# Written orders for the end of the attention and the gating, and normalised rows turned through memory and VectorE

## The chip, the cores and the metric

One core of one Trainium2 chip runs the whole program in one launch. The metric is the device time in microseconds (us). The kernel before was run three times: 1278.26, 1278.86 and 1281.36 us, with a median of 1278.86. One further execution was profiled.

The engines are called PE (TensorE), DVE (VectorE), ACT (ScalarE), POOL (GpSimd) and SP (SyncE, which here only issues DMAs). Each engine executes its own instructions in order, and waits in that order.

## What is computed

The input is `x` of 4 x 16 x 16 x 1024, that is 1024 tokens of 1024 channels (float32). Two layers follow each other:

```
x = x + conv_attn(group_norm(x))          # layer 0: q, k, v, a 256x256 map per head and batch
t = tokens(x)                             # 4 x 256 x 1024
t = t + attention(layer_norm(t))          # layer 1: 16 causal heads, then W_proj and b_proj
h = layer_norm(t)
g = softmax(h @ gate_w + gate_b)          # 8 experts
w = g * (g >= 0.1); w = w / sum(w)
t = t + sum_e w[:, e] * (h @ expert_w[e] + expert_b[e])
```

So there are two layer norms over tokens, and after each the rows are needed transposed: channels on the partitions, tokens along the free axis, since a matrix product on PE contracts over the partitions.

## The kernel before

The 1024 tokens are eight tiles of 128 (`NT = 8`, `P = 128`), and the 1024 channels are eight chunks (`NC = 8`). Everything is float32. A matrix product with 512 columns is recorded as two 128x512 matmul records of 0.43 us each, so that one step over a chunk takes 0.86 us of PE. Unless something else is said, the order of the instructions on each engine is chosen by the scheduler of the framework, which may move an instruction ahead of others. Inside `tc.manual_schedule()` the order of the text is the order on each engine; with a set of engines given, only for these.

**End of layer 0 (lines 432 to 453).** For each of eight tiles `content` makes one part of the map (matmuls `pc`, line 342, added on DVE in line 350), and 16 matmul records `py` (line 443) multiply it with the values; DVE adds `py` onto the tile of x (line 450). Then `layer_norm` (line 155): statistics on DVE, a root on ACT, the normalised row written by ACT (line 166), eight transposes on PE (line 170) into PSUM, and two ACT copies of these into `ln1` (line 171), which is the transposed operand of the next layer. POOL adds the bias `bp` (line 452), and SP writes the row to `x_rows` in memory, from where it comes back later.

**Attention (lines 457 to 703).** `project_v` makes the values from `ln1`. Two-by-two block products with seven instead of eight multiplications are used here and for q and k: DVE makes sums of blocks first (`sums_of_A`, `sums_of_B`), and PE then makes the seven products `pqk` (line 492). The heads go in eight pairs, and four batches make 32 steps `(pair, b)`. A step consists of:

- `scores` (line 573): four matmuls into the one buffer `sc`; DVE adds the mask and writes `s` (line 593), two maxima on DVE (line 605), four exponentials on ACT, the reciprocal of their sums on DVE (line 614), four products on POOL (line 617). SP then writes the weights, laid out by quarters, to memory (line 623) and reads them back in four pieces (line 627).
- three steps later (`lag = 3`) `turned` (line 632): one DVE transpose by blocks of 32x32, which together with the trip through memory gives the full transpose; and `values` (line 638), eight matmul records, with a bias added on DVE into `y_T` (line 651).

Into these steps the dictionary `units` places the products of the next pair's q and k, and `out_at` places six pieces of the output projection `project_out` (line 658, matmuls `po` in line 663, added onto x on DVE in line 666) in steps 28 to 33. In step 27 eight reads `x_rows` to `xb` go out on SP (line 697). The whole loop is in the scheduler's order.

**Gating (lines 797 to 1028).** The ten other pieces of the output projection, 80 chunks of 0.86 us, run while the rows of x go through a chain of stages, which the dictionary `after` places by halves of pieces: `normalise` (stage 0: statistics, root, the row on DVE in line 863, eight transposes on PE in line 845, a copy of one half on ACT and of the other on DVE, and a write of the row, laid out by quarters, to `rows`, from which the experts' rows are gathered), `gate` (stage 1: 16 matmul records `parts` for the gates, a copy, a matmul `pg`, and some ten small DVE instructions with one exponential on ACT), `place` (stage 2: the place of each token in its experts' lists) and `enter` (stage 3: matmuls into `lists`). SP writes x to `out` after stage 0. Before the stages, DVE makes a number of constants (lines 804 to 839), and SP issues the two halves `w0` of the first expert's weights, 2 MB each, and its bias (lines 984 and 985). At the end `read_lists` turns the list of expert 0 into addresses.

**Experts (from line 1194 on).** This stage has a written order already. The last tile is multiplied by expert 0 as a whole (`weighted`, line 750, called `dense`), while POOL gathers the rows of the first list by indirect DMAs (line 735), DVE turns them by `turn` (line 745), and then the products of the experts follow.

Of the kernel before, what the change touches and what calls it, by code (L numbers as in the profile page):

```python
# [32 lines left out]
F32 = mybir.dt.float32  # L33
I32 = mybir.dt.int32
AF = mybir.ActivationFunctionType
ALU = mybir.AluOpType
# [31 lines left out]
def kernel(  # L68
# [86 lines left out]
    def layer_norm(ln, t, dst):  # L155
# [8 lines left out]
        less = small.tile([P, 1], F32, tag="ln_less", name=f"ln1_less{t}")  # L164
        nc.vector.scalar_tensor_tensor(less, mv[:, 0:1], -1.0, rstd, ALU.mult, ALU.mult)
        nc.scalar.activation(ln, xs[t], AF.Identity, bias=less, scale=rstd)  # L166
        for j in range(2):
            pt = tr(f"ln1_pt{t}_{j}")
            for c in range(4):
                nc.tensor.transpose(pt[:, ts(c, P)], ln[:, (4 * j + c) * P : (4 * j + c + 1) * P], ident)  # L170
            nc.scalar.copy(dst[:, 4 * j : 4 * j + 4, ts(t, P)], pt.rearrange("p (c n) -> p c n", c=4))


    with ExitStack() as layer0:
# [253 lines left out]
        ln1 = big_tile(1, "ln1")  # L428
        ln_rows = wpool.tile([P, 4, C], F32, tag="w", name="ln_rows")
        bp = ln_rows[:, 3, :]  # L430
        nc.gpsimd.dma_start(bp, b_proj.partition_broadcast(P))
        for i, (b, nt) in enumerate(tiles):
            if i == 0:
                content(b, nt)
            if i + 1 < NT:
                content(*tiles[i + 1])
            t = 2 * b + nt
            for hp in range(2):
                py = mm(f"py{t}_{hp}")
                for hl in range(2):  # L440
                    bh = b * HEADS0 + 2 * hp + hl
                    for mh in range(2):
                        nc.tensor.matmul(  # L443
                            py[:, ts(hl, M)],
                            s0[:, mh, ts(nt, S2), :, bh].rearrange("p i j -> p (i j)"),
                            v_T[:, mh, ts(b, M)],
                            start=(mh == 0),
                            stop=(mh == 1),
                        )
                nc.vector.tensor_add(xs[t][:, ts(hp, HALF)], xs[t][:, ts(hp, HALF)], py)  # L450
            layer_norm(ln_rows[:, i % 3, :], t, ln1)
            nc.gpsimd.tensor_add(xs[t], xs[t], bp)  # L452
            nc.sync.dma_start(x_rows[ts(t, P), :], xs[t])
# [3 lines left out]
    with ExitStack() as attention:  # L457
# [41 lines left out]
        def project_v(r):  # L499
# [18 lines left out]
            for t in range(4):  # L518
                nc.scalar.copy(homes(t)[1], one(t, 3, s4, b22))
# [829 lines left out]
```

## Time and profile before

| | |
|---|---|
| runs | 1278.26, 1278.86, 1281.36 us |
| profiled execution, its own time | 1278.4 us |
| its span | 1276.6 us |
| mean granted clock of PE | 0.991 |
| PE, DVE busy | 98%, 54% of the span |
| ACT, POOL busy | 17%, 27% |
| q1 (the queue of the plain loads and writes) | 27.3% of 16 engines' span |
| end of layer 0, gating | about 224 to 293 us, about 690 to 780 us |

The profile is of one execution. Its span, from the first to the last instruction, lies 1.8 us below the time of that execution. A line such as `L845 PE MATMUL row_pt<-ident,row ... x64 | 9.4, 295 | 4.9 <-DVE row L863 4.9` is a group: line of the kernel, engine, operation, what it writes and reads, how many, then busy time in us and the mean of one in ns, then the idle time of the engine just before these instructions and what ended it. Times of matmuls overlap, so a mean in ns is not what one of them costs on a full PE. A row of the windows gives start:end, length, busy time of each engine with the number of instructions, the granted clock of PE (1.00 is full), the share of the DMA engines and their GB/s. In the chain of waits each row has a start, a length, and the engine and line, or the DMA, that held the end back.

### The profile page before, as it was taken

The numbers are of one execution on the slowest core, as the hardware profiler recorded it, in microseconds if no ns is written. First come the engines' busy times: TensorE is split into PE (matmuls) and PEld (weight loads), VectorE is DVE, ScalarE is ACT, GpSimd is POOL, SyncE is SP. The second block draws the span as 40 slices with busy tenths as digits, with TensorE's granted clock in tenths as the row PEclk, the third lists the DMA queues.
The fourth block names the chain that finished last, engine by engine and source line by source line (L and its number), as shares of the span: only waits on it lengthen the run. The fifth ranks groups of instructions, "written<-read, shape, count | busy, mean of one in ns | idle before, by whom it ended". The sixth has DMA issues, their size and how long they took to land.

```text
span 1276.6 us, 12809 instructions
## 1 busy us (share of the span) xinstructions
PE 1248.8 (98%) x4646; PEld 657.0 (51%) x4646; DVE 694.6 (54%) x1297; ACT 221.6 (17%) x520; POOL 350.0 (27%) x423
## 2 busy tenths in 40 slices
PE   9999999999999999999889998999999999999997
PEld 5444895788884444444434544444344434433443
DVE  5784220566322666665545754755656665665642
ACT  3300111231000222222221322011111110111110
POOL 0000051230000222222210011554644544363520
PEclk9999999999999999999889998999999999999999
DMA  9020022612202535353744415274658375557442
GB/s 353 7 66 2 16 63 70 232 65 99 67 1 66 153 102 163 108 168 99 246 137 154 174 50 210 71 232 89 185 150 232 90 231 154 141 118 210 99 82 51
DMA packets 83605, 159.76 MB, mean 125 GB/s; under 512 B 8368, under 2 KB 39104, under 8 KB 83536
## 3 DMA queue, kind: packets, MB, share of 16 engines
q1 hardware_dynamic: 70704, 119.49, 27.3%
q0 software_dynamic: 12832, 39.39, 14.0%
q8 instruction: 38, 0.62, 0.2%
q14 instruction: 31, 0.25, 0.1%
HBM read 109.30 MB, written 45.35 MB: 121 GB/s over the span
## 4 chain that ended last, share of the span: by engine, by line
PE 75%; issue 13%; POOL 5%; DVE 3%; DMA 3%; ACT 0%; SPq 0%; POOLq 0%; ACTq 0%; DVEq 0%
PE p L1120 29%; PE po L663 7%; PE pq L259 7%; PE pv L492 7%; POOL s_q L617 5%; PE left L1162 3%; PE pT L378 3%; PE pqk L492 3%; PE py L443 2%; PE pk L321 2%; PE pc L342 2%; PE pv L403 2%; PE rest L1176 2%; PE last_pe L1274 1%; DMA s_rows<-s_q 1%
## 5 line engine op out<-in xcount | busy, mean ns | idle before, releaser
L735 POOL DMA_INDIRECT w_e_xg<-rows,gather x146 | 155.2, 1063 | 67.5 <-issue 41.7
L1120 PE MATMUL p<-w_e,A 128*128 128x512 f32 x368 | 163.2, 593 | 1.8 <-DVE slot L981 1.8
L617 POOL TENSOR_TENSOR s_q<-s_q,total 128x128 f32<-128x128 f32 (+1 forms) x128 | 65.3, 541 | 301.9 <-DVE total L614 301.9
L663 PE MATMUL po<-w_p,y_T 128*128 128x512 f32 x256 | 119.5, 613 | 0.0
L1120 PEld LDWEIGHTS p<-w_e,A 128*128 128x128 f32 x368 | 69.6, 190 | 90.4 <-issue 89.9
L1120 PE MATMUL p<-T,S 128*128 128x512 f32 x256 | 112.7, 593 | 0.0
L1126 ACT ACTIVATE y<-y,slot 128x512 f32<-128x512 f32 x64 | 46.0, 721 | 336.3 <-DVE y L1134 183.9
L763 POOL DMA_INDIRECT out_dram<-y,add x32 | 57.4, 1794 | 171.0 <-ACT y L1126 110.1
L259 PE MATMUL pq<-w_q,xn 128*128 128x512 f32 x224 | 99.6, 596 | 1.4 <-DVE q_s L263 1.1
L607 ACT ACTIVATE s_q<-s,top 128x256 f32<-128x256 f32 (+1 forms) x128 | 56.6, 443 | 182.6 <-issue 143.1
L492 PE MATMUL pqk<-ln,w_qk 128*128 128x512 f32 x192 | 86.0, 596 | 0.0
L1120 PEld LDWEIGHTS p<-T,S 128*128 128x128 f32 x256 | 48.6, 190 | 60.8 <-issue 60.7
L663 PEld LDWEIGHTS po<-w_p,y_T 128*128 128x128 f32 x256 | 47.5, 195 | 52.1 <-issue 51.9
L745 DVE STREAM_TRANSPOSE A<-w_e_xg 128x1024 f32<-128x1024 f32 x32 | 39.6, 1238 | 59.8 <-DMA w_e_xg<-rows,gather 56.6
L259 PEld LDWEIGHTS pq<-w_q,xn 128*128 128x128 f32 x224 | 41.8, 190 | 51.8 <-issue 47.4
L492 PE MATMUL pqk<-T,S_qk 128*128 128x512 f32 x128 | 58.3, 598 | 0.0
L492 PEld LDWEIGHTS pqk<-ln,w_qk 128*128 128x128 f32 x192 | 35.8, 190 | 42.7 <-issue 41.5
L1120 PE MATMUL p<-w_e,S 128*128 128x512 f32 x128 | 57.5, 592 | 0.0
L1120 PE MATMUL p<-T,A 128*128 128x512 f32 x128 | 57.5, 592 | 0.0
L492 PE MATMUL pv<-w_v,ln 128*128 128x256 f32 x192 | 43.4, 379 | 0.0
L1162 PE MATMUL left<-w_e,one 128*32 128x512 f32 x312 | 41.8, 593 | 0.0
L452 POOL TENSOR_TENSOR x_at<-x_at,ln_rows 128x1024 f32<-128x1024 f32 x8 | 19.4, 2429 | 76.6 <-ACT ln_rows L166 76.6
(265 smaller groups left out, 1781.0 us busy)
## 6 DMA issues: line engine op xcount, KB each, us to landing
w_e<-in_expert_w_dram SPq DMA_DIRECT2D x16, 2048.0 KB, 12.2
s_rows<-s_q SPq DMA_DIRECT2D x32, 384.0 KB, 2.5
s_rows<-s_rows SPq DMA_DIRECT2D x128, 96.0 KB, 2.4
w_qk<-in_W_attnT_dram SPq DMA_DIRECT2D x8, 1024.0 KB, 6.1
xn<-in_xT_dram SPq DMA_DIRECT2D x8, 512.0 KB, 5.8
x_at<-in_x_dram SPq DMA_DIRECT2D x8, 512.0 KB, 8.5
w_v<-in_W_attnT_dram SPq DMA_DIRECT2D x2, 2048.0 KB
x_rows<-x_at SPq DMA_DIRECT2D x8, 512.0 KB, 2.7
```

The lines of the kernel that those rows point to most:

```text
L259: nc.tensor.matmul(pq, xn[:, c, ts(t, P)], w_q[kc][:, c, :], start=(c == 0), stop=(c == NC - 1))
L378: nc.tensor.matmul(out_T[:, g, :, :], window[:, kc, :, :].rearrange("p i j -> p (i j)"), q0[:, kc, first : first + n_i, nj, :], start=(kc ...
L492: nc.tensor.matmul(bank, stationary(c), moving(c), start=(c == 0), stop=(c == NC // 2 - 1))
L607: nc.scalar.activation(blocks(h, qt), s[:, h, cols].rearrange("p (b f i) -> p b f i", f=Q, i=32), AF.Exp, bias=top[:, qt, h : h + 1], accu ...
L617: nc.gpsimd.tensor_mul(blocks(h, qt), blocks(h, qt), total[:, qt, h : h + 1].unsqueeze(2).unsqueeze(3).to_broadcast([P, 1 + qt, Q, 32]),)
L663: nc.tensor.matmul(po, y_T[:, c, ts(t, P)], w_p[j][:, c, :], start=(c == 0), stop=(c == NC - 1))
L735: nc.gpsimd.indirect_dma_start(out=row[:, g, :], out_offset=None, in_=table[: (TOK - P) * Q, :] if e in SHORT else table, in_offset=bass.I ...
L745: nc.vector.transpose(row_T[:, :, :slots].rearrange("p c (g j) -> p g c j", j=32), row[:, : slots // 32, :].rearrange("p g (c i) -> p g c ...
L763: nc.gpsimd.indirect_dma_start(out=out[: TOK - P, :] if e in SHORT else out, out_offset=bass.IndirectOffsetOnAxis(ap=add[:slots, e, k : k ...
L1120: nc.tensor.matmul(bank, a[:, c, :], b[:, c, :], start=(c == 0), stop=(c == NC // 2 - 1))
L1126: nc.scalar.mul(y[i][:, ts(j, HALF)], y[i][:, ts(j, HALF)], slot[:, e, 1, 2 * pair + i : 2 * pair + i + 1])
L1162: nc.tensor.matmul(bank[ts(i, 32), :], stationary, w[of][j][:, c, :], start=(c == 0), stop=(c == NC - 1))
```

## The change

Four things change.

1. **Layer 0.** `layer_norm` no longer transposes on PE. ACT writes the normalised row in the order of quarters, SP writes it to memory and reads it back by `quarters_of` in four pieces, and one DVE `turn` puts it into `ln1`. The write of `x_rows` moves from SP to POOL's queue. In this loop SP's instructions are in the written order. `project_v` takes the tiles in the order 1, 3, 0, 2 for products 1, 2 and 3, and its sums wait for the last tile's normalisation.
2. **Attention, steps 22 to 34.** They are in a written order on all engines. The scores of a step are split: `scores` ends with the exponentials, `scored` holds the rest. The sums of pair 7 (`sums_qk`) are made in step 22, units stand ahead of or behind the values and scores, the pieces of the output projection take the values and scores after their seventh chunk, the second half of `w_p` is loaded in step 28, and the reads of x are issued from POOL, two per step in steps 28 to 31.
3. **Gating.** It is in a written order on all engines, and `after` counts single chunks. For tiles 0 to 5 the row is written by ACT in quarter order, goes to memory and back by `quarters_of`, and is turned on DVE; tiles 6 and 7 keep the transposes on PE. The stages are six: `normalise`, `turn_rows`, `gate_sums`, `gate`, `place`, `enter`.
4. **Between gating and experts.** The address list is spread by PE before the last tile's statistics are made, 14 matmuls whose result is not used stand behind that, and the dense tile takes the stages of tile 7 and two sums of blocks of the weights between its chunks.

The diff, cut to its core:

```diff
+    def normalised(row, of, mean, rstd):
+        less = small.tile([P, 1], F32, tag="ln_less", name="ln_less")
+        done = nc.vector.scalar_tensor_tensor(less, mean, -1.0, rstd, ALU.mult, ALU.mult)
+        nc.scalar.activation(
+            row.rearrange("p (f c i) -> p c f i", f=Q, c=NC),
+            of.rearrange("p (c f i) -> p c f i", c=NC, f=Q),
+            AF.Identity, bias=less, scale=rstd)
+        return done
+
+    def quarters_of(rows, home, name):
+        row = home.tile([P, Q, C // Q], F32, tag="xg", name=name)
+        for f in range(Q):
+            nc.sync.dma_start(row[ts(f, 32), :, :], rows[:, f, :].rearrange("(g j) c -> j g c", j=32))
+        return row
...
-    def layer_norm(ln, t, dst):
+    def layer_norm(ln, t, dst, home, turns):
...
-        nc.scalar.activation(ln, xs[t], AF.Identity, bias=less, scale=rstd)
-        for j in range(2):
-            pt = tr(f"ln1_pt{t}_{j}")
-            for c in range(4):
-                nc.tensor.transpose(pt[:, ts(c, P)], ln[:, (4 * j + c) * P : (4 * j + c + 1) * P], ident)
-            nc.scalar.copy(dst[:, 4 * j : 4 * j + 4, ts(t, P)], pt.rearrange("p (c n) -> p c n", c=4))
+        done = normalised(ln, xs[t], mv[:, 0:1], rstd)
+        rows = turns.tile([P, Q, C // Q], F32, tag="rows", name=f"ln1_rows{t}")
+        nc.sync.dma_start(rows.rearrange("n f c -> n (f c)"), ln)
+        turn(dst[:, :, ts(t, P)], quarters_of(rows, home, f"ln1_quarters{t}"))
+        return done
...
+        with tc.manual_schedule(engines={mybir.EngineType.SP}):
...
+                ln_done = layer_norm(ln_rows[:, i % 3, :], t, ln1, tpool, turns)
+                nc.gpsimd.tensor_add(xs[t], xs[t], bp)
+                nc.gpsimd.dma_start(x_rows[ts(t, P), :], xs[t])
...
+            with tc.issue_after(ln_done.ins):
+                sums_of_A(*a, s1, s2, s4)
...
+        units = {
+            22: ([(6, 4), (6, 5)], []),
+            23: ([], [(7, 1)]),
+            24: ([(7, 2)], [(7, 6)]),
+            25: ([(7, 7), (7, 4)], []),
+            26: ([(6, 3)], [(7, 5)]),
+            27: ([(7, 3)], []),
+        }
+        out_at = {28: (0, 0), 29: (1, 0), 30: (0, 1), 31: (1, 1), 32: (2, 0), 33: (2, 1)}
+        with tc.manual_schedule():
+            for i in range(written, len(steps) + lag):
+                if i == written:
+                    w_p.append(w_tile("w_p0", W_projT[:, :HALF]))
+                if i == 28:
+                    w_p.append(w_tile("w_p1", W_projT[:, HALF:]))
...
+                if 28 <= i < 32:
+                    for t in range(2 * (i - 28), 2 * (i - 28) + 2):
+                        nc.gpsimd.dma_start(xs[t], x_rows[ts(t, P), :])
+                s_T = turned(*steps[i - lag], soft.pop(i - lag))
+                ahead, behind = units.get(i, ((), ()))
+                for unit in ahead:
+                    project_qk(*unit)
+
+                def values_and_scores():
+                    values(*steps[i - lag], s_T)
+                    return scores(*steps[i]) if i < len(steps) else None
+
+                made = []
+                if i in out_at:
+                    project_out(*out_at[i], {NC - 2: lambda: made.append(values_and_scores())})
+                else:
+                    made.append(values_and_scores())
+                if i == written:
+                    sums_qk(7)
+                for unit in behind:
+                    project_qk(*unit)
+                if made[0]:
+                    soft[i] = scored(*steps[i], *made[0])
...
-            nc.vector.tensor_scalar(row, xs[t], mv[:, 0:1], rstd, ALU.subtract, ALU.mult)
+            if t < NT - 2:
+                normalised(row, xs[t], mv[:, 0:1], rstd)
+                nc.sync.dma_start(rows[ts(t, P), :], row)
+                row = quarters_of(rows[ts(t, P), :].rearrange("n (f c) -> n f c", f=Q), l2w, f"quarters{t}")
+            else:
+                nc.vector.tensor_scalar(row, xs[t], mv[:, 0:1], rstd, ALU.subtract, ALU.mult)
+            nc.sync.dma_start(out[ts(t, P), :], xs[t])
+            return row
...
         after = {
-            0: (0, 2, 4, 6),
-            1: (2, 4, 6, 8),
...
+            0: (1, 11, 13, 14, 19, 24),
+            1: (3, 20, 22, 23, 28, 33),
+            2: (12, 29, 31, 32, 37, 42),
+            3: (21, 38, 40, 41, 46, 51),
+            4: (33, 47, 49, 50, 55, 60),
+            5: (49, 59, 61, 62, 67, 72),
+            6: (65, 69, 71, 72, 76, 79),
         }
...
+        with tc.manual_schedule():
+            for t in range(3, NT):
+                for j in range(2):
+                    project_out(t, j, {c: one_more for c in range(NC)})
+            entries = copy_lists(0)
+            pc = spread_lists(0, entries)
+
+            warm = tr("warm")
+            for _ in range(14):
+                nc.tensor.matmul(warm[:, :P], before, ones, start=True, stop=True)
+            stage(0, NT - 1)
+            take_lists(0, 1, pc)
+            stage(1, NT - 1)
...
-            first_sum(0)
-            second_sum(0)
-            bias_step(0)
...
-                {0: lambda: stage(2, NT - 1), 1: lambda: (put(0, 0), put(0, 1), row_sums(0, 0))},
+                {
+                    (0, 3): lambda: stage(2, NT - 1),
+                    (0, 4): lambda: (stage(3, NT - 1), first_sum(0)),
+                    0: lambda: (stage(4, NT - 1), put(0, 0)),
+                    (1, 3): lambda: put(0, 1),
+                    1: lambda: (row_sums(0, 0), second_sum(0), bias_step(0)),
+                },
```

## The prediction

> **What bounds the kernel now.** I read the busy shares, then the slices with the granted clock, then the windows around the places where the clock drops, then the groups of the instructions that leave, and last the chain of waits.
>
> ```profile
> PE 1248.8 (98%) x4646; PEld 657.0 (51%) x4646; DVE 694.6 (54%) x1297; ACT 221.6 (17%) x520; POOL 350.0 (27%) x423
> ...
> PEclk9999999999999999999889998999999999999999
> ```
>
> PE is busy 98% of the span, so only two things can pay: fewer PE instructions, and the places where PE waits or runs at a low clock. The digits 8 mark the second kind. The windows (length, then busy time of PE, PEld, DVE, ACT, POOL, then the granted clock, DMA share, GB/s) show them closely:
>
> ```profile
> 620.00:630.00 10.00, 5.95 (x34) 3.21 (x34) 7.18 (x13) 3.72 (x16) 3.34 (x8) 0.97 0.52 171
> 630.00:640.00 10.00, 10.00 (x26) 4.42 (x27) 3.08 (x6) 1.86 (x8) 2.35 (x5) 0.69 1.00 339
> ...
> 655.00:660.00 5.00, 3.44 (x11) 1.70 (x12) 3.83 (x7) 3.09 (x9) 2.05 (x5) 0.50 0.46 141
> 660.00:690.00 30.00, 30.00 (x91) 13.03 (x91) 9.07 (x19) 0.46 (x3) 1.56 (x4) 1.00 0.23 78
> ...
> 782.00:790.00 8.00, 6.89 (x32) 4.12 (x33) 4.05 (x15) 1.63 (x2) 0.00 (x0) 0.57 1.04 391
> ```
>
> PE stands still and then computes at half clock. By the matmul records the half clock holds three times for 6.83 us (629.36, 653.25, 782.96), each time after some 3 to 4 us of idle. Against the rate of undisturbed stretches (0.86 us for one 128x512 product step, which is two records of 0.43) I count 8.0 us lost at 624-636, 7.6 at 650-660, 8.2 at 778-791, 1.4 at 694-697 and 1.5 near 290. All other stretches are packed to within 0.2 us per change of shape.
>
> The instructions that leave PE:
>
> ```profile
> L845 PE MATMUL row_pt<-ident,row 128*128 128x128 f32 x64 | 9.4, 295 | 4.9 <-DVE row L863 4.9
> L170 PE MATMUL ln_pt<-ident,ln_rows 128*128 128x128 f32 x64 | 8.5, 275 | 1.4 <-ACT ln_rows L166 1.4
> ```
>
> Their busy time overlaps; in the chain of waits eight of them take 0.87 to 0.93 us, 0.11 us each. The 4.9 us beside the first group is PE waiting for a normalised row.
>
> The chain between 617 and 656 names what held PE in the attention:
>
> ```profile
> 626.49 5.51 DMA xb<-x_rows
> ...
> 634.01 9.03 DMA s_rows<-s_q
> ...
> 655.54 0.98 DVE s_T L632
> ```
>
> The eight 512 KB loads of x (626 to 634) and the weighted rows of the scores share SP's queue; a trip that otherwise takes 2.3 us took 9.03, so the values came late.
>
> **A, the end of layer 0.** Removed: 64 transposes x 0.109 = 7.0 us of PE, 16 ACT copies (0.59 each, beside PE), and PE's wait for the last row, 1.5. Added per tile, all beside PE: a 512 KB write, four quarter reads, a turn on DVE. Nearest rows:
>
> ```profile
> L745 DVE STREAM_TRANSPOSE A<-w_e_xg 128x1024 f32<-128x1024 f32 x32 | 39.6, 1238 | 59.8 <-DMA w_e_xg<-rows,gather 56.6
> ...
> s_rows<-s_rows SPq DMA_DIRECT2D x128, 96.0 KB, 2.4
> ...
> x_rows<-x_at SPq DMA_DIRECT2D x8, 512.0 KB, 2.7
> ```
>
> The trip of a row: ACT 1.24, write 2.7, four issues some 1.75 and landing 2.4, turn 1.24, about 9.3 us. PE's tile falls from 7.86 us (3.44 pc, 3.55 py, 0.87 transposes) to 6.99. DVE's tile is six 0.69 us instructions for adds and statistics and 0.7 of small ones, 4.8; with the turn 6.06 of 6.99. So DVE fits at 87%, and a turn is hidden as long as it doesn't wait in front of the adds. Behind a turn that waits stand, on DVE, the next adds of py and pc, and PE waits for these once its banks are full; behind a quarter read that waits for its write stands on SP only the next row. The x_rows write moves to POOL, which is nearly idle here (4.0 of 13 us at 270-283). The values' projection takes t = 1, 3, 0, 2, so the last tile's trip has four products before it is needed (about 292 against 298). Range 8.5 gained to 12 lost (below); I take 7 gained, 1.5 kept back for DVE's 87%.
>
> The Trainium skill, "VectorE: DVE Perf Modes", sections "The three transpose paths" and "Rules for kernel authors", speaks against this: a full 128x128 transpose belongs on TensorE, 390 ns each, since VectorE turns only 32x32 blocks. At 390 ns the 112 transposes removed in all would be worth 44 us; the rows here price them at 12.6, and the four reads by quarters supply what the blocks lack.
>
> **B, attention steps 22 to 34.** Freed: the two losses, 15.6 us, since the x loads go to POOL's queue two per step and the scores no longer stand two in a row. POOL issues the loads between the products with the reciprocal (L617), which take 2 x 0.63 + 2 x 0.42 = 2.1 us of a step of some 8. New waits, from the written order of DVE: in step 23 values(20) need turned(20), which stands behind s(22) 0.95, two reductions 0.68 + 0.41, sums_qk(7) 0.98 + 0.74 + 0.67 + 0.67, the reciprocal 0.17 and its own 0.97. That is 6.2 us in which PE has no other unit, as (7,1) stands behind the scores; behind the turn DVE holds the y_T add and s(23), which PE needs only later. An idle of 3 us has cost a half-clock spell of 6.83, some 3 us; together 9.2. Smaller: scores(26) behind the adds of (7,7) and (7,4) 0 to 1.5; w_p1, issued at step 28 and needed at step 30, 0 to 3 (the 2 MB of w_p took 8.4 us for both halves and now share the queues with x); the last values 0 to 1.8. I take 2 of these 6.3. B gains 15.6 - 11.2 = 4.4; bounds 12 gained (no wait at step 23, were it covered) to 0 gained (all waits).
>
> **C, gating until the last chunk.** Removed: 48 transposes, 5.6 us, and the 1.4 us wait for the first row, 7.0. DVE loses row 0.81 and copy 0.69 per tile and gains a turn of 1.24, so its load (48.4 of 82 us in 700-782) doesn't grow. The new wait is gate_sums(0) at chunk 13, due 13 x 0.86 = 11.2 us after the attention. Its chain: constants on DVE 3.8 (691.6 to 695.4), statistics and root 2.3, ACT 1.24, write 2.6 (by_quarter's quiet landing), quarter reads 4.15, turn 1.24: 15.3. So 4.1 us idle when the queues are quiet. Before, the first by_quarter write, behind 4 MB of w0, needed some 13.5 us instead of 2.6, which would make it 15. Now w0's first half may go before the attention ends and the second (8 us alone) is nearly through when the write starts at 7.3; I take 5 idle and 3 of half clock. Seven more places where PE meets DVE (pg, gate_sums, place of t = 0 to 6) wait 0 to 9 us in all by the same kind of sum; as DVE's load doesn't grow I take 2. C loses 3; bounds 7 gained, 20 lost.
>
> **D, end of gating and dense.** The last tile still goes over PE. Of the 8.2 us, the 3.7 of idle are now filled with list spreading and 14 small products at about 0.22 us, 3.05, which should keep the clock up. Freed is thus the half-clock part and what the gather gains by starting earlier (last output projection to first product 25.1 us before, some 20 to 21 after). 5 gained; bounds 0 and 8.
>
> **Sum** against the profiled execution: 1278.4 (span 1276.6 and 1.8 around it) - 7 - 4.4 + 3 - 5 = **1265.0**; the median of the runs is 0.5 higher, which I neglect.
>
> **Rivals.**
> 1. The written orders bring no new wait: 8.5 + 12 + 7 + 8 = 35.5 gained, **1243**. For it: DVE is at 54%. Against: step 23, where nothing on PE covers 6.2 us.
> 2. The first gating rows meet w0: SP issues the row's write behind w0's second half and bias0 (SP stood 4.9 us at bias0, 692.5 to 697.5). Idle 15 + 3 instead of 5 + 3 and the small waits 5 instead of 2: 1265 + 13 = **1278**, no change. It decides if gate_sums(0) comes over 15 us late.
> 3. **Slower**: in layer 0 the turn of tile t stands on DVE right behind the next tile's normalisation and waits there for its trip: 1.24 + 2.7 + 4.15 = 8.1 us after the root, less 4.8 of DVE work between, leaves 3.3 us per tile. DVE's tile becomes 6.06 + 3.3 = 9.4 us against PE's old 7.86: 1.5 x 8 = 12 lost in place of 7 gained, 1265 + 19 = **1284**. It decides once DVE's tile, wait and all, is over 8.7 us. For it: DVE executes in order. Against: only SP's order is written out there, so the turn can be placed two tiles later.
> That the change doesn't do what it says can be excluded for the 112 transposes (the code goes), not for the waits.
>
> **How the numbers follow.** Forecast (some waits stay, 1254 to 1274) 0.46; rival 1 (under 1254) 0.19; rival 2 (1274 to 1282) 0.17; rival 3 0.18. About 0.3%, 3.8 us, is what a measurement can tell from no change, so the same is 1275.0 to 1282.7. Faster: 0.46, 0.19 and 0.02 of rival 2, 0.67; same: 0.15 of rival 2 and 0.02 of rival 3, 0.17; slower: 0.16 of rival 3. The range, 1241 to 1287, reaches from rival 1 to rival 3 with 3 us of its small waits; outside lie 0.08 of rival 3, where the turn waits longer, and 0.05 of rival 1.
>
> **What would show it.** A: no ln_pt, DVE near 87% between 224 and 290, PE without idle. B: an idle of PE of about 6 us before the values of step 23 with a digit 8 or lower after it, none at the x loads. C: PE waiting for the first turn some 11 us after the attention, 5 us long. D: clock 1.00 through the dense tile. Wrong would make it: PE idle in layer 0 on DVE, more than two half-clock spells, or none.

## The result and the profile after

The changed kernel takes 1301.13 us (1300.08 to 1302.71), against 1278.64 for the kernel before in the same comparison: a ratio of 1.017, with a 95% interval of 1.0153 to 1.0187. It is 1.7% slower. The profiled execution took 1300.31 us with a span of 1298.5.

The busy shares and the clock of the slices of the page after:

```profile
PE 1245.8 (96%) x4562; PEld 650.9 (50%) x4562; DVE 709.9 (55%) x1303; ACT 214.7 (17%) x502; POOL 358.0 (28%) x439
...
PEclk9999999999999999998989899999999999999999
```

PE has 84 matmul records fewer (112 of the transposes left, and 28 of the 14 unused products came), and yet it is busy for only 3.0 us less in a span that is 21.9 us longer. There are still three digits 8. So the work went, and new waits came. The waits of PE after, with the total, the count and the longest one:

```profile
PE pv L519 <- DVE ln L178: 10.0, 2, 8.1
PE pa L683 <- DVE s_T L671: 8.5, 3, 5.8
PE parts L945 <- issue: 7.7, 1, 7.7
PE po L701 <- DMA w_p<-in_W_projT_dram: 5.8, 1, 5.8
PE pn L1123 <- DVE U L1213: 2.8, 1, 2.8
PE parts L945 <- DVE row_T L178: 2.4, 4, 0.8
```

From the same list of the kernel before:

```profile
PE sc L579 <- DVE s L593: 5.6, 3, 3.0
PE row_pt L845 <- DVE row L863: 4.9, 2, 3.7
PE pa L644 <- DVE s_T L632: 3.5, 1, 3.5
...
PE pn L1042 <- DVE U L1132: 0.6, 1, 0.6
```

So the groups `pa` and `pn` waited before too, for less and, in the case of `pa`, at another step; the other four rows of the list after are new. Its third row has no engine's name, but it ends when the first turn of the gating on DVE ends (719.54 against 719.64). The windows show what followed each of the five longest waits; the columns are those of before:

```profile
283.00:300.00 17.00, 7.93 (x26) 6.00 (x24) 10.94 (x11) 1.88 (x3) 4.89 (x4) 0.70 0.51 167
...
590.00:600.00 10.00, 4.24 (x26) 2.15 (x26) 7.18 (x12) 1.86 (x8) 2.42 (x6) 0.90 0.24 79
600.00:609.00 9.00, 9.00 (x27) 4.43 (x24) 3.61 (x6) 2.55 (x9) 1.98 (x5) 0.74 0.30 102
655.00:663.00 8.00, 2.21 (x17) 1.04 (x13) 4.20 (x7) 1.86 (x8) 2.96 (x6) 0.77 1.01 387
663.00:670.00 7.00, 7.00 (x13) 3.19 (x14) 0.00 (x0) 0.00 (x0) 0.00 (x0) 0.77 0.90 266
711.00:720.00 9.00, 1.26 (x11) 0.46 (x13) 1.71 (x2) 0.00 (x0) 0.00 (x0) 0.67 0.70 252
720.00:728.00 8.00, 8.00 (x32) 3.80 (x24) 4.35 (x21) 4.31 (x5) 0.00 (x0) 0.74 0.57 198
840.00:846.00 6.00, 1.60 (x12) 1.42 (x11) 3.91 (x9) 0.00 (x0) 0.14 (x1) 0.81 0.09 29
846.00:853.00 7.00, 6.94 (x11) 3.03 (x12) 4.98 (x12) 0.72 (x1) 1.62 (x1) 0.68 0.00 0
```

In the first four places PE is idle for 6 to 8 us, in the last for 2.8 and then 1.6 us, and where it works again the granted clock is down. The 0.74 to 0.77 of the windows are averages: in windows cut to the spell itself (597.92 to 604.75, for example) the clock is 0.50, for 6.83 us in three of the places and for 10.24 us in two. Five such places stand where the kernel before had three.

The program can be cut by the first and last matmul of a name, and the pieces add up to the whole. All times are us of PE:

| piece | before | after | |
|---|---|---|---|
| start to first py | 228.4 | 229.2 | +0.8 |
| first to last py (end of layer 0) | 54.4 | 49.1 | -5.3 |
| last py to last pv (values' projection) | 100.1 | 110.2 | +10.1 |
| last pv to last pa (attention) | 307.7 | 312.1 | +4.4 |
| last pa to last po (gating) | 88.9 | 99.2 | +10.3 |
| last po to first expert product | 24.5 | 22.4 | -2.1 |
| first product to last matmul | 466.3 | 470.7 | +4.4 |

The sum is 22.6; the stretch after the last matmul is 0.8 shorter, which leaves the 21.9 (rounded) of the span.

### The profile page after: what moved, and what is told of

Read it like the earlier page. It is cut to its first block, busy times and chain, and to the rows that moved or that the text cites. A ratio compares the mean times of both kernels' runs of the same rounds, so it can differ in the third digit from the quotient of the medians.

```text
span 1298.5 us, 12774 instructions
## 1 busy us (share of the span) xinstructions
PE 1245.8 (96%) x4562; PEld 650.9 (50%) x4562; DVE 709.9 (55%) x1303; ACT 214.7 (17%) x502; POOL 358.0 (28%) x439
## 3 DMA queue, kind: packets, MB, share of 16 engines
q0 software_dynamic: 15136, 47.78, 15.6%
## 4 chain that ended last, share of the span: by engine, by line
PE 42%; DVE 3%; issue 2%; DMA 2%; POOL 1%; ACT 1%; SPq 0%; DVEq 0%; POOLq 0%; ACTq 0%
PE p L1201 29%; PE po L701 6%; PE left L1243 3%; PE rest L1257 2%; PE last_pe L1358 1%; DMA w_p<-in_W_projT_dram 1%; DMA w_e_xg<-rows,gather 1%; POOL w_e_xg L802 1%; PE pqk L519 1%; PE pa L683 1%; DVE ln_stats L907 0%; DVE row_T L178 0%; PE sc L614 0%; PE parts L945 0%; POOL out_dram L1296 0%
## 5 line engine op out<-in xcount | busy, mean ns | idle before, releaser
L701 PE MATMUL po<-w_p,y_T 128*128 128x512 f32 x256 | 122.5, 619 | 5.8 <-DMA w_p<-in_W_projT_dram 5.8
L519 PEld LDWEIGHTS pv<-w_v,ln 128*128 128x128 f32 x192 | 37.8, 198 | 16.2 <-issue 10.7
```

The source lines that it names most:

```text
L519: nc.tensor.matmul(bank, stationary(c), moving(c), start=(c == 0), stop=(c == NC // 2 - 1))
L701: nc.tensor.matmul(po, y_T[:, c, ts(t, P)], w_p[j][:, c, :], start=(c == 0), stop=(c == NC - 1))
```

## The experiments

My theory after these traces: the loss is a sum of separate waits, each with a cause of its own: in layer 0 the turned tiles come late; in step 23 the values wait for a turn behind other DVE work; at step 30 the second half of the projection's weights has not landed; the gating's first row meets the first expert's weights; and behind the dense tile a sum on DVE delays a gather. The rival to each is written with the run. Each kernel was run beside the kernel before, whose median was 1279.9 to 1280.8 in these comparisons, against 1278.6 in that of the change. So the ratios are the safer guide, and a microsecond or two between two medians of the table says little. The pieces and waits below are from one profiled execution of each kernel.

| kernel | median us | ratio to before | 95% interval |
|---|---|---|---|
| the change | 1301.13 | 1.0170 | 1.0153 to 1.0187 |
| undo_layer0 | 1298.05 | 1.0142 | 1.0125 to 1.0158 |
| turn_order | 1299.88 | 1.0150 | 1.0133 to 1.0167 |
| layer0_half | 1295.19 | 1.0122 | 1.0101 to 1.0143 |
| unit_ahead | 1296.27 | 1.0130 | 1.0113 to 1.0147 |
| out_order | 1293.00 | 1.0101 | 1.0084 to 1.0118 |
| late_w0 | 1292.37 | 1.0099 | 1.0081 to 1.0117 |
| late_w0_stage | 1293.88 | 1.0109 | 1.0090 to 1.0127 |
| early_sums | 1294.65 | 1.0114 | 1.0096 to 1.0132 |
| all_five | 1279.82 | 0.9994 | 0.9977 to 1.0011 |
| all_pinned | 1269.12 | 0.9919 | 0.9901 to 0.9937 |
| steps_alone | 1270.66 | 0.9928 | 0.9911 to 0.9944 |
| half_and_steps | 1268.79 | 0.9905 | 0.9888 to 0.9921 |
| all_mended | 1267.06 | 0.9899 | 0.9884 to 0.9914 |
| all_mended_spread | 1269.54 | 0.9916 | 0.9903 to 0.9930 |

### Layer 0

**undo_layer0**: the end of layer 0 of the kernel before, put into the changed one.

```diff
-        done = normalised(ln, xs[t], mv[:, 0:1], rstd)
-        rows = turns.tile([P, Q, C // Q], F32, tag="rows", name=f"ln1_rows{t}")
-        nc.sync.dma_start(rows.rearrange("n f c -> n (f c)"), ln)
-        turn(dst[:, :, ts(t, P)], quarters_of(rows, home, f"ln1_quarters{t}"))
...
+        nc.scalar.activation(ln, xs[t], AF.Identity, bias=less, scale=rstd)
+        for j in range(2):
+            pt = tr(f"ln1_pt{t}_{j}")
+            for c in range(4):
+                nc.tensor.transpose(pt[:, ts(c, P)], ln[:, (4 * j + c) * P : (4 * j + c + 1) * P], ident)
...
-            with tc.issue_after(ln_done.ins):
-                sums_of_A(*a, s1, s2, s4)
+            sums_of_A(*a, s1, s2, s4)
...
-            in_time = (1, 3, 0, 2)
+            in_time = range(4)
```

> The changed kernel with the end of layer 0 as it was (transposes on PE, free order, x_rows from SP, tiles 0 to 3 in order). Theory: the part from the start to the end of the values' projection took 159.3 us against 154.5 before, so this gives back 4.8 us: 1301.1 becomes about 1296. PE's waits for turned tiles (8.1, 2.0 and 0.9 us near 285 to 312) are gone. Rival: what layer 0 loses is taken up later anyway, or the attention is late because of it; then it stays at 1301 or falls below 1292.

The last pv ends at 382.9 instead of 388.5, and the rest of the program takes as long as it did. The median falls by 3.1 us only, and the intervals of the two ratios overlap a little; that layer 0 of the change lost time rests on the pieces of the traces. But why? DVE between 286 and 307 in the trace after (start, length, what):

```profile
286.03 3.35 DVE L153 TENSOR_TENSOR w_v<-w_v 128x1024 f32<-128x1024 f32 x1
289.31 1.23 DVE L178 STREAM_TRANSPOSE ln<-ln_quarters 128x1024 f32<-128x1024 f32 x1
...
291.90 1.22 DVE L178 STREAM_TRANSPOSE ln<-ln_quarters 128x1024 f32<-128x1024 f32 x1
...
299.53 1.23 DVE L178 STREAM_TRANSPOSE ln<-ln_quarters 128x1024 f32<-128x1024 f32 x1
...
305.05 2.36 DVE L178 STREAM_TRANSPOSE ln<-ln_quarters 128x1024 f32<-128x1024 f32 x2
```

Five of the eight turns come after the last py (278.2). The quarters of the first of these had landed at 270.7 by the records of the DMA issues, 18.6 us earlier; DVE had it behind the adds and the sums of the values' weights, of which the one in line 153 took 3.35 us instead of 1.2 (the last section returns to it). With two quarter buffers, the reads of a tile wait for the turn two tiles earlier, and SP, in its written order, holds the next row's write behind these reads: one write was issued at 277.66, the next only at 292.39.

**turn_order**: DVE in the written order too, with the turn of a tile two tiles later.

```diff
-        turn(dst[:, :, ts(t, P)], quarters_of(rows, home, f"ln1_quarters{t}"))
-        return done
+        quarters = quarters_of(rows, home, f"ln1_quarters{t}")
+        return done, lambda: turn(dst[:, :, ts(t, P)], quarters)
...
-        with tc.manual_schedule(engines={mybir.EngineType.SP}):
+        to_turn = []
+        with tc.manual_schedule(engines={mybir.EngineType.SP, mybir.EngineType.DVE}):
...
-                ln_done = layer_norm(ln_rows[:, i % 3, :], t, ln1, tpool, turns)
+                ln_done, turn_it = layer_norm(ln_rows[:, i % 3, :], t, ln1, tpool, turns)
+                to_turn.append(turn_it)
+                if i >= 2:
+                    to_turn.pop(0)()
...
+            for turn_it in to_turn:
+                turn_it()
```

> The changed kernel with DVE in written order in the last loop of layer 0: the turn of a tile stands two tiles later and all turns stand ahead of the sums of the values' weights. Theory: the turns came up to 18 us after their quarters had landed because DVE had them behind other work, and with two quarter buffers this held SP's reads and the next rows; PE's 11 us of waiting and the half clock shrink to the trip of the last tile, about 1297. Rival: the trip of the last tiles is itself too long for what PE has left after the last py, whatever DVE does: 1300 to 1302, or slower if a turn now waits in front of the adds.

The median is 1299.88, 1.3 below the change, and the intervals overlap. PE's wait stays, in the window 262 to 320:

```profile
PE pv L525 <- DVE ln L178: 7.5, 1, 7.5
```

The gain that I expected did not come. DVE now turned the fourth tile 17 us earlier (272.52), and yet PE waits nearly as long. But DVE did not get the order that the edit was meant to give, since instructions of the next block of the program stand between those of this one. DVE sits for 4.5 us (279.5 to 284.0) at an add of the values' projection (line 549) and turns the fifth tile only behind it; and the sums of the weights stand ahead of the sixth turn (289.2 to 296.3), although the text has the turns first. It is this sixth turn that PE waits for, and one of its quarters had landed at 281.56. The py piece came out 3.4 us longer than in the change (52.5), the values' projection 5.0 shorter (105.2). So the run does not tell the two causes apart, DVE's late turns and the length of the trip. The next one takes the last tiles off this way, and with them both causes.

**layer0_half**: the first four tiles through memory, the last four on PE.

```diff
+        if on_pe:
+            less = small.tile([P, 1], F32, tag="ln_less", name="ln_less")
+            done = nc.vector.scalar_tensor_tensor(less, mv[:, 0:1], -1.0, rstd, ALU.mult, ALU.mult)
+            nc.scalar.activation(ln, xs[t], AF.Identity, bias=less, scale=rstd)
+            for j in range(2):
+                pt = tr(f"ln1_pt{t}_{j}")
...
+            return done
...
-                ln_done = layer_norm(ln_rows[:, i % 3, :], t, ln1, tpool, turns)
+                ln_done = layer_norm(ln_rows[:, i % 3, :], t, ln1, tpool, turns, i >= 4)
```

> The changed kernel, where only the first four tiles of the end of layer 0 go through memory and DVE, and the last four are transposed on PE as before. Theory: what was lost is the trip of the last tiles, for which PE has no other work left; the first four are covered, so 4 x 0.87 = 3.5 us of PE are gained against before and the 4.8 us lost come back: 1301.1 - 8.3, about 1293. Rival: it is DVE's load in the loop that costs: 1298 to 1301.

The last pv ends at 380.2, 8.3 us ahead of the change and 2.7 ahead of the kernel before; the py piece is 50.8, 3.6 below before, as 4 x 0.87 says. (The median falls by 5.9 only: the attention, the gating and the stretch behind it are 0.7 to 1.3 us longer in this trace, and the kernel before was 2.1 us slower in this comparison.) PE waits 1.2 and 0.5 us in place of 10.0. So the way through memory is worth its place as long as py work follows it, and not for the last tiles in the order that this kernel has. DVE's load alone did not cost this: it is the same per tile in the first four. How much of the tail's loss a DVE order that keeps to the turns would save, no run shows.

### The attention's steps

**unit_ahead**: something for PE to do while the turn of step 23 is on its way.

```diff
-            22: ([(6, 4), (6, 5)], []),
-            23: ([], [(7, 1)]),
+            22: ([(6, 4)], []),
+            23: ([(6, 5)], [(7, 1)]),
```

> The changed kernel with unit (6, 5) ahead of the values of step 23 instead of step 22. Theory: PE's 6.0 us of idle before the values of step 23 shrink by its 3.4 us to about 2.6, too short for a half-clock spell (3 us): about 1295. Rival: the wait only moves to the next step, since DVE is as late there: 1299 to 1301.

1296.27. The wait at the values of step 23 is now, in the window 580 to 610:

```profile
PE pa L683 <- DVE s_T L671: 2.1, 1, 2.1
```

The attention takes 306.1 us instead of 312.1: 3.7 us of waiting and some 2.3 of half clock are gone, and nothing came at the next step: in the windows 588 to 600 and 600 to 610 the clock is 1.00. The theory held.

**out_order**: the order of the pieces of before.

```diff
-        out_at = {28: (0, 0), 29: (1, 0), 30: (0, 1), 31: (1, 1), 32: (2, 0), 33: (2, 1)}
+        out_at = {28: (0, 0), 29: (1, 0), 30: (2, 0), 31: (0, 1), 32: (1, 1), 33: (2, 1)}
```

> The changed kernel with the pieces of the output projection in the order (0,0) (1,0) (2,0) (0,1) (1,1) (2,1), so that the second half of its weights is needed one step later. Theory: the 6.0 us wait for it at 656.6 and the half clock after it (some 2.5) go: about 1293. Rival: the loads are late because six x loads share the queues with it, and the wait moves one step on or to the adds of x: 1298 to 1301.

1293.00, as expected. In the change the chain between 650 and 664 is one transfer:

```profile
650.05 12.90 DMA w_p<-in_W_projT_dram
```

The 2 MB shared the queues with four of the x loads (645 to 662) and landed at 662.95; PE had nothing else from 657.2 on. One step later it is there, and the window 630 to 700 has no wait for it. The attention takes 304.0 instead of 312.1.

### The gating

**late_w0**: the second half of the first expert's weights and the bias are needed only by the dense tile, some 90 us later; here they go out after chunk 51.

```diff
-        w0 = [half_weights(0, r, w_even) for r in range(2)]
-        bias0 = expert_bias(0, l2w)
+        w0 = [half_weights(0, 0, w_even)]
+        bias0 = None
...
+            if chunks == 51:
+                w0.append(half_weights(0, 1, w_even))
+                bias0 = expert_bias(0, l2w)
```

> The changed kernel with the second half of the first expert's weights and its bias issued after chunk 51 of the gating instead of at its start. Theory: the first row, ready at 706.9, landed at 713.8 because 2 MB of weights were in the queues; quiet it takes 2.6 us, so the turn comes 4.3 us earlier and PE's wait of 7.7 us shrinks to about 3.5, without the half-clock spell: about 1294. Rival: the constants of DVE and the trip itself set the wait: 1300.

1292.37, a little more than expected: the gating takes 89.3 us instead of 99.2. The transfers of the window 695 to 720 after show the contention (KB each, median us to landing):

```profile
w_e<-in_expert_w_dram SPq DMA_DIRECT2D x1, 2048.0 KB, 10.1
rows<-row SPq DMA_DIRECT2D x2, 512.0 KB, 7.8
w_e_bias<-in_expert_b_dram SPq DMA_DIRECT2D x1, 512.0 KB, 10.9
```

My expectation had named the wrong row: the one at 706.9 is the second tile's. The first tile's row was ready at 687.3 in the change, since the scheduler had put its normalisation between the last steps of the attention. It was written late all the same, at 702.43, because SP stood from 693.19 to 701.11 at the weights' second half, whose buffer the attention still held; then the write took 11.4 us to land (713.78). In late_w0 the write goes out at the same moment, 702.29 (there ACT makes the row only at 701.02), and its quarters are read from 705.48 on: some 3.2 us. The difference of 8.2 us is the contention, and it covers PE's wait of 7.7, which is gone altogether. What remains of waits between 698 and 790 is small:

```profile
PE parts L945 <- DVE row_T L178: 2.5, 4, 0.8
...
PE lists L1013 <- DVE entry L1002: 1.0, 1, 1.0
PE pg L953 <- DVE sums L947: 0.6, 1, 0.6
PE pp L979 <- DVE g_keep L966: 0.3, 1, 0.3
```

**late_w0_stage**: the same, and `0: (1, 16, 18, 19, 24, 29)` in `after` instead of `0: (1, 11, 13, 14, 19, 24)`.

> As the last one, and the stages of tile 0 from the turn on stand five chunks later (16, 18, 19, 24, 29 for 11, 13, 14, 19, 24). Theory: the rest of the wait, some 3.5 us, is covered by 4.3 us of chunks: about 1291. Rival: DVE is then late for tile 1, and the wait moves there: as the last one.

1293.88, and the gating 91.4: no gain, rather 2 us lost in this piece, while the two intervals overlap. There was nothing left to cover, and the later stages of tile 0 now fall between those of tile 1 (waits of 1.4 at a turn and 1.4 at the lists are new). I had overrated the wait that remained.

### Behind the dense tile

**early_sums**: the first two sums of the weights and the bias step ahead of the dense tile.

```diff
+            first_sum(0)
+            second_sum(0)
+            bias_step(0)
             for k in range(3):
                 get(0, k)
...
-                    (0, 4): lambda: (stage(3, NT - 1), first_sum(0)),
+                    (0, 4): lambda: stage(3, NT - 1),
...
-                    1: lambda: (row_sums(0, 0), second_sum(0), bias_step(0)),
+                    1: lambda: row_sums(0, 0),
```

> The changed kernel with the first two sums of the first expert's weights and the bias step ahead of the dense tile, as before the change. Theory: behind the dense tile the second sum (2.3 us on DVE) stood ahead of the add that lets POOL send the dense rows and then gather the fourth group; without it the gather lands earlier, PE's 2.8 us wait at 841 falls to about 0.6 and the half clock after it (3 us) goes: about 1296. Rival: the gathers start late by the address list itself, and the wait stays: 1300 to 1302.

1294.65; the stretch from the first product on takes 465.2 instead of 470.7, and the 2.8 us wait is not in the list any more. The theory held. The scheduler put the two sums at 711.8 to 716.4, where DVE stood waiting for the first row of the gating, so that they cost nothing here.

### Together

**all_five** holds undo_layer0, unit_ahead, out_order, late_w0_stage and early_sums.

> All of it: the end of layer 0 as before, unit (6, 5) in step 23, the pieces in the order of before, the late load with tile 0 five chunks later, and the early sums. Theory: the places are apart, so the gains add up: 1301.1 - 4.8 - 6 - 8 - 10 - 5 = about 1267, faster than before. Rival: waits that are hidden behind these come out, and it stays near 1280.

1279.82, 0.9994 of before: some 13 us slower than the sum, in ten runs from 1273.6 to 1284.2. The trace shows a new place. DVE in the gating of this kernel:

```profile
755.37 1.28 DVE L907 BATCH_NORM_STATS2 ln_stats<-xb 128x6 f32<-128x512 f32 x2
756.56 2.28 DVE L1147 TENSOR_TENSOR T<-w_e,w_e 128x2048 f32<-128x2048 f32 x1
...
758.88 2.29 DVE L1150 TENSOR_TENSOR T<-w_e,T 128x2048 f32<-128x2048 f32 x1
...
761.70 0.81 DVE L918 TENSOR_SCALAR row<-xb,ln_mv,ln_rstd 128x1024 f32<-128x1024 f32 x1
```

The two sums of the weights, which stand in the text behind the gating, run between the statistics and the row of tile 6. The written order holds inside its block; the first instructions of the next block may be put in between those of the block before. PE waited 4.2 us for that row.

**all_pinned**: the same kernel, with these sums tied to the last DVE instruction of the gating.

```diff
-            nc.vector.tensor_copy(add[:, a:b, :], slot[:, a:b, 0, :])
+            return nc.vector.tensor_copy(add[:, a:b, :], slot[:, a:b, 0, :])
...
-            take_lists(0, 1, pc)
+            taken = take_lists(0, 1, pc)
...
-            first_sum(0)
-            second_sum(0)
-            bias_step(0)
+            with tc.issue_after(taken.ins):
+                first_sum(0)
+                second_sum(0)
+                bias_step(0)
```

> The kernel with all five edits, where the first two sums of the expert's weights and the bias step may be issued on DVE only after the last address of the first list. Theory: in the kernel with five edits the scheduler put these two sums (2.28 and 2.29 us) between the statistics and the row of tile 6, and PE waited 4.2 us for that row; pinned, this wait goes: 1279.8 becomes about 1275. Rival: they cost as much at the new place, 1279.

1269.12, more than twice the gain expected. The gating went from 97.1 to 91.3 us, the stretch to the first product from 26.5 to 23.4, and the products from 467.9 to 465.3. The edit moved one thing, so these all hang on where the two sums and the bias step stand. The traces hold most of it. In the gating the wait of 4.2 us is gone, and with it a spell of 3.41 us at half clock. In the stretch behind it waits of 1.1 at `pg` and 1.7 for a turned gather are gone, and among the products another such spell.

**steps_alone**: the kernel before, with the written steps 22 to 34 and the edits of unit_ahead and out_order, and nothing else.

> The kernel before with only the written steps 22 to 34 of the change, mended by the two edits (unit (6, 5) in step 23, the pieces in the order of before); layer 0, gating and experts as before. Theory: the part from the end of the values' projection to the last values took 298.2 us in the kernel with all five edits against 307.7 before, so this part alone gains 9.5 us: 1279.9 becomes about 1270. Rival: the gating of before needs its start as it was and gives the gain back: 1277 or more.

1270.66, ratio 0.9928 (0.9911 to 0.9944). The attention takes 299.6 us against 307.7. This part, mended, is faster by itself.

**half_and_steps**: steps_alone with the layer 0 of layer0_half.

> Layer 0 with four tiles through memory and four on PE, and the mended steps 22 to 34; gating and experts as before the change. Theory: 9.5 and 3.5 us gained, 1279.9 becomes about 1267, the fastest. Rival: the two disturb each other or one of them does not hold: 1272 or more.

1268.79, ratio 0.9905. Layer 0 adds some 2 us, less than the 3.5 that I gave it, and the interval overlaps with that of steps_alone.

**all_mended**: layer0_half, unit_ahead, out_order, late_w0 and the pinned sums in the changed kernel.

> The changed kernel with every mended place at once: four tiles of layer 0 through memory and four on PE, unit (6, 5) in step 23, the pieces in the order of before, the late load of weights with the stages of tile 0 where the change has them, and the pinned early sums. Theory: with the load out of the way the written gating takes 89.3 us, as in the run with the late load, so the whole is 380.3 to the end of the values' projection, 298.2, 89.3, some 23 and 465.2, and 7.5 around it: about 1264, a little faster than the kernel that keeps the gating of before (1268.8). Rival: the gating loses again in this company, as with the shifted stages (91.3), and it is no faster than 1268.8.

1267.06, ratio 0.9899 (0.9884 to 0.9914), the fastest measured. It is 1.0% faster than before. Against half_and_steps it is 1.7 us lower, with overlapping intervals: the gating takes 89.3 us here and 89.1 there. So the written gating with its 48 transposes less is worth nothing measurable, even with the load out of its way: in half_and_steps, with the gating of before, PE does not wait in this piece at all, and here it waits 4.4 us. The last piece took 469.8 us and not the 465.2 of my sum. The profile has 1.3 us of waiting at `pn` again, 1.8 behind it, and from 811.44 on 6.83 us at half clock; all_pinned, with 465.3, has only a wait of 1.6 there and no such spell. What makes that turn late again is open.

**all_mended_spread**: one chunk more between a turn and the gate sums, for tiles 0 to 5.

```diff
-            0: (1, 11, 13, 14, 19, 24),
-            1: (3, 20, 22, 23, 28, 33),
+            0: (1, 11, 14, 15, 20, 25),
+            1: (3, 20, 23, 24, 29, 34),
...
```

> The same with the gate sums of tiles 0 to 5 three chunks after the turn instead of two, and gate, place and enter of these tiles one chunk later too. Theory: what holds the gating at 89 us although 48 transposes (5.6 us) have left PE is that the gate sums follow their turn by 1.72 us only, and PE waits 0.4 to 0.9 us for the turn of each tile, 2.5 us together; one chunk more takes most of it: 2 us faster than the last one, about 1262. Rival: the waits are DVE's and move to the gate and the lists: within 1 us of the last one.

1269.54: the theory fell. The waits for the turns fall from 2.5 to 2.1 us only, those at `pg` rise from 0.6 to 1.9, and the gating takes 90.1 us. The waits are DVE's, and move with it. The gating accounts for 0.9 of the 2.5 us by which this kernel is slower; 1.7 more lie in the attention, which the edit does not touch (299.9 instead of 298.2). There the wait of 2.1 us at the values of step 23 was followed by 3.41 us at half clock, where the same wait in all_mended was not.

## Why the prediction was wrong, point by point

The forecast was 1265.0, faster; the kernel came out at 1301.13, outside the range of 1241 to 1287. All four terms failed, by 11.8 (layer 0), 8.8 (attention), 7.3 (gating) and 7.3 us (end), together 35.2 of the 35.3 us between 1265.0 and the 1300.3 of the profiled execution.

**Layer 0, 7 gained.** Measured: 4.8 lost in the two pieces of the edit. The removal was right: the py piece fell by 5.3 us. The step that failed is "the last tile's trip has four products before it is needed (about 292 against 298)". The last turns ended at 307, and PE, which now finished py 4.6 us sooner, came to them earlier still. I had priced the trip of one tile, 9.3 us, and not the queue of five tiles at the end: two quarter buffers, SP's order and DVE's order put them one behind the other. The trip itself was underpriced too: the write of a row took 3.6 to 7.8 us (median 4.6) where I had 2.7, a quarter read 3.0 where I had 2.4. Which of these costs most, no run separates. For layer0_half, where this tail is taken away, the layer gains 2.7. My third rival had the engine and the place right but the mechanism the other way round: DVE did not wait in front of the adds; the turns were put too late.

**Attention, 4.4 gained.** Measured: 4.4 lost. The large new wait was right: 6.2 us predicted at the values of step 23, 5.8 measured, with a half clock after it. The old losses of 15.6 went. Mis-sized was the term "I take 2 of these 6.3": the weights cost 5.8 us of waiting, above its bound of 3, and with the half clock behind it 8.1 by out_order; the values of step 26 (not the scores, as I had it) waited 1.1 us and the last values 1.7. That makes 10.9 in place of 2, which is the size of the miss (8.8). I had the row of 2 MB in 8.4 us and wrote that it shares the queues with x, and still did not add the sharing: it took 12.9. I had also misread the row, which is of one half of `w_p` and not of both.

**Gating, 3 lost.** Measured: 10.3 lost. The place of the wait, chunk 13, was right, and its size near (7.7 us for 5), but not for my reasons. The chain with its 3.8 us of constants was not the one: the first row was ready before the attention ended. The step that failed is that the second half of the weights "is nearly through when the write starts at 7.3": the write started at 702.43, 1.9 us after the last values, and met the whole of the weights and the bias. My bound for this, 13.5 us for the write, was close to the 11.4 measured. The small waits took 4.3 instead of 2. My second rival named this mechanism; late_w0 shows it, with 9.9 us of the 10.3 in this piece.

Also wrong was the other side of the sum. Of the "7.0" removed, nothing shows when the load is out of the way (89.3 against 88.9): 4.4 us stand in the list of small waits, and part of tile 6's later stages now falls into this piece. How the last 2 us or so divide between these and the more frequent changes of shape on PE, no run tells.

**End of gating and dense, 5 gained.** Measured: 2.1 gained to the first product (22.4 after 24.5; I had 25.1 and some 20 to 21) and 4.4 lost after it. The clock stayed up through the dense tile as forecast. What I had not looked at is what the moved sum does behind it: second_sum (2.28 us) stood on DVE ahead of the add after which POOL sends the dense rows, and POOL's next gather, then DVE's turn, then PE came late by as much. I wrote of the gather's earlier start and did not follow its order on POOL to the fourth group.

**The rivals.** Each put its price on one mechanism. What happened is that all of the places went towards their bad ends at once, and the attention and the end beyond them (both had 0 gained as the worst bound). The 12 gained that rival 1 has for the attention is not worked out anywhere: without a new wait the term is the 15.6 of the old losses.

The Trainium skill ("VectorE: DVE Perf Modes", section "Rules for kernel authors") puts a full 128x128 transpose on TensorE where the result may go to PSUM. That comes out right for the last tiles of layer 0; in the gating the turns through memory gained nothing (89.3 us against 89.1), and the four hidden tiles of layer0_half did gain. The price that its section "The three transpose paths" gives, 390 ns, is for bf16: of the float32 transposes here eight in a row took 0.87 us in most places, and a turn of eight blocks took 1.24 us as in the trace before.

## What to carry to other kernels

Taking work off a full PE pays only as long as PE has other work while the longer way is travelled: look at the last tiles of a loop first, since there nothing follows. When an order is written by hand, list for each wait what PE has in hand, and fill the largest with a unit that is already there; two entries in a dictionary were worth 5 and 8 us here. Move every load that isn't needed soon behind the small transfers that are, and tie the first instructions behind a written block to its end.

## What the runs showed of the hardware

Idle times of PE of 6 to 8 us were followed by a spell of 6.83 or 10.24 us in which the granted clock was 0.50, and so was the idle of 2.8 us at 841 with 1.6 us more behind it (6.83 us from 843.68). Around 2 us the traces go both ways: after a wait of 2.1 us the clock stayed at 1.00 in unit_ahead and all_mended and was 0.50 for 3.41 us in all_mended_spread, and two waits of 1.0 us shortly after each other were followed by such a spell in all_pinned (774.33) and by none in the change. A 512 KB write took 2.6 to 2.7 us alone and 11.4 us from issue to landing beside a load of 2 MB (702.4 to 713.8).

One DVE add of 128x1024 in layer 0 (line 153) took 3.35 us in the trace after and 1.16 in the trace before. It ran beside POOL's add of the last row of x (285.04 to 288.30), which itself took 3.26 us where the others took 2.36. The kernel before has the same at another of these adds: line 151 took 2.79 us beside an add of POOL that took 2.91 (283.97 to 286.88). A DVE instruction of one column (line 159, usually 0.16 us) took 2.12 us and ended within 0.02 us of the end of POOL's add beside it (283.49). So the two engines held each other up in these places; adds of py, which come from PSUM, took their usual 0.69 us beside an add of POOL.
